# Holding back small bfloat16 products and telling a list scheduler what a change of product kind costs, in a two-layer graph attention kernel

## The chip, the cores and the metric

The kernel runs on one core of one Trainium2 chip. The metric is device time in microseconds (us) of one execution. The time before is the median of seven runs, 916.81 us (912.74 to 923.02).

## The reference, cut to what matters

The input is a dense matrix `adj` of 2708 x 2708 in which few entries are not zero (the diagonal, and entries that grow denser towards low row and column numbers), and features `x` of 2708 x 256. Two layers follow each other. Layer 0 is a gated graph layer:

```python
node_support = node_adj_norm @ h                      # one plain aggregation
edge_output = _gru_cell(node_support, h, ...)
for each of 3 heads:                                  # _gat_head
    att = softmax(where(edge_adj > 0, e_plus, where(edge_adj < 0, e_minus, NEG_INF)), axis=1)
    edge_support += att * edge_adj @ (h @ W)
node_output = _gru_cell(edge_support / 3, h, ...)
x = layernorm(x + de * edge_output + dn * node_output)
```

Every softmax row has its denominator: the sum of the weights `exp(e)` over the entries of that row that are not zero, for each of the three heads. Layer 1 is an ordinary graph attention layer with four heads and a mask `adj > 0.5`, with a second layernorm behind it.

## The kernel before, in words

The kernel never multiplies with the whole matrix. It reads the matrix once, finds which rows hold anything in each block of columns, and then gathers only those rows. There are three stretches of work.

*Reading and listing* (first 240 us or so). SyncE loads `adjT` in blocks of 128 x 512 (tile `at`). ScalarE makes sign masks from it (`over`, `mask`, bfloat16), VectorE finds the non-empty rows (`f_found`), TensorE multiplies the masks in bfloat16 into banks `acc` and `db`. Between them TensorE also makes float32 products of `x` with the GRU weights, which are kept for later (`keep`). `listed` and `spread` turn the found rows into lists of row numbers (`f_idx`), with small bfloat16 products into banks `ls` and `pl`.

*Layer 0.* The columns are cut into 43 chunks of 64, and each chunk into "tiles" of up to 128 listed rows: 181 tiles in all, 163 of them gathered. For a tile n, `fetch_raw` brings the 128 x 64 entries of `adjT` and `fetch_rows` the 128 x 264 rows of features and weights (ring `rows`), each by an indirect DMA that GpSimd (POOL) issues. `prepared` makes `four` (the entries times 1 and times the three heads' weights, float32) and the mask `m0` (sign, bfloat16; its rows in the profile carry the short name `m`). `multiplied` makes two float32 products per tile into the bank `sums[c]` (acc; the profile records four matmuls for these two products) and one small bfloat16 product of mask and weights, 128 x 64 by 128 x 9, into the bank `dens[c]` (db): the denominators. There are two banks of each kind, taken in turn by the chunks. After the last tile of a chunk `divided` sums and inverts the denominators on VectorE, spreads them with one float32 product (`rden_own`) and scales the chunk. After every eight chunks (512 columns) `cells_and_norm` runs the GRU cells: 12 products with `f_gat_w`, 24 for each cell (half of that where `keep` has done a part), transposes, the layernorm, and the projection for layer 1, whose rows go to a table in DRAM.

*Layer 1.* Once its table is written, 91 gathered tiles (indirect DMAs into the same ring `rows`) are weighed on VectorE, multiplied in float32 and finished. The masks of these tiles are 91 further indirect DMAs of 128 x 128 entries (`fetch_mask`, tile `raw1`, in the profile `raw<-in_adj_dram`). They need only the lists, so they can be issued during layer 0.

The order of the instructions on each engine isn't that of the source. Class `Plan` records every instruction, and `Plan.issue` is a list scheduler: it gives each recorded operation a cost from `Plan.cost`, follows the dependencies that buffers make, and at each step lets the engine that is free first issue the ready operation with the longest remaining chain (`tail`). What it decides is written into the program; on the chip each engine then works through its queue in that order. All instructions of the fast path therefore stand at one line in the profile, L208. A general path for other inputs stands behind a branch and doesn't run.

Consecutive TensorE instructions with the same output bank are joined to one operation of the scheduler (up to 16 of them). The cost of a product before is one line:

```python
t = max(0.06, n / 2000) if ins[0].dtype == BF16 else max(0.22, n / 590)
```

Of the kernel before, what the change touches and what calls it, by code (L numbers as in the profile page):

```python
# [11 lines left out]
BF16 = mybir.dt.bfloat16  # L12
# [8 lines left out]
P = 128  # L21
# [4 lines left out]
C1 = D // HEADS1  # L26
# [15 lines left out]
W0 = 64  # L42
# [54 lines left out]
class Plan:  # L97
# [8 lines left out]
    ENGINES = ("tensor", "vector", "scalar", "gpsimd", "sync")  # L106
    LAG = 0.08
    LOAD, RATE, QUEUED = 2.2, 250.0e3, 4.0
    TABLES = {AF.Sigmoid: 1, AF.Tanh: 1, AF.Exp: 2, AF.Sqrt: 3}

    def __init__(self, nc):
# [36 lines left out]
    def cost(self, engine, method, out, ins, kwargs):  # L148

        n = max(self.count(v) for v in [out] + ins)  # L150
        if method == "indirect_dma_start":
            return 1.25, 3.0
        if method == "dma_start":
            size = 4
            for _, k in tuple(out.ap):
                size *= k
            return 0.08 if engine == "sync" else 0.25, self.LOAD + size / self.RATE
        if engine == "tensor":
            n = self.count(out)
            t = max(0.06, n / 2000) if ins[0].dtype == BF16 else max(0.22, n / 590)  # L160
            return t, t + 0.1
        by_partition = any(isinstance(kwargs.get(k), bass.AP) for k in ("bias", "scale"))
        if engine == "scalar":
            t = 0.09 + n / 1200 + 0.1 * by_partition
        elif engine == "gpsimd":
            t = 0.1 + n / (1300 if method == "memset" else 320)
        elif method == "reciprocal":
            t = 0.07 + n / 160
        else:
            pairs = all(v.dtype == BF16 and tuple(v.ap)[-1] == (1, 2) for v in [out] + ins)  # L170
            t = 0.06 + n / (1900 if pairs else 3800 if method == "memset" else 960)
            t += 0.065 * (method == "scalar_tensor_tensor")
        return t, t + 0.08

    def note(self, engine, method, f, args, kwargs):
        found = list(args) + list(kwargs.values())
        found = [v.ap if isinstance(v, bass.IndirectOffsetOnAxis) else v for v in found]
        found = [v for v in found if isinstance(v, bass.AP)]
        out, ins = found[0], found[1:]
        writes = [out] + ([kwargs["accum_out"]] if kwargs.get("accum_out") is not None else [])  # L180
        n, deps = len(self.ops), set()

        last = self.ops[-1] if n else None
        joined = (
            engine == "tensor" and n and last.engine == engine and last.out == out.tensor.name
            and len(last.calls) < self.JOINED
        )
        n -= joined
        for v in found:
            t = self.touched(v)  # L190
            if t is None:
                continue
            name, p0, p1, m = t
            w = any(v is o for o in writes)
            old = self.seen.setdefault(name, [])
            keep = []
            for other in old:
                k, q0, q1, mo, wo = other
                if (w or wo) and k != n and p0 < q1 and q0 < p1 and m & mo:
                    deps.add(k)  # L200
                    if w and p0 <= q0 and q1 <= p1 and not mo & ~m:
                        continue
                keep.append(other)
            keep.append((n, p0, p1, m, w))
            self.seen[name] = keep
        busy, done = self.cost(engine, method, out, ins, kwargs)
        table = self.TABLES.get(args[2] if method == "activation" else None, 0)
        call = lambda: f(*args, **kwargs)  # L208
        if joined:
            last = self.ops[n]  # L210
            deps.discard(n)
            last.calls.append(call)
            last.deps |= deps
            last.busy += busy
            last.done += busy
            return
        self.ops.append(Op(engine, [call], busy, done, table, deps, method, self.urgent, out.tensor.name))

    def issue(self):
        ops, total = self.ops, len(self.ops)  # L220
        after = [[] for _ in ops]
        for n, op in enumerate(ops):
            for k in op.deps:
                after[k].append(n)
        tail, urgent = [0.0] * total, [op.urgent for op in ops]
        for n in reversed(range(total)):
            op = ops[n]
            for m in after[n]:
                tail[n] = max(tail[n], tail[m] + (0.0 if ops[m].engine == op.engine else self.LAG))
                urgent[n] = max(urgent[n], urgent[m])  # L230
            tail[n] += op.done
        tail = [t + u for t, u in zip(tail, urgent)]
        left = [len(op.deps) for op in ops]
        start = [0.0] * total
        free = dict.fromkeys(self.ENGINES, 0.0)
        ready = {e: [] for e in self.ENGINES}
        for n, op in enumerate(ops):
            if not left[n]:
                ready[op.engine].append(n)
        moved, table = 0.0, 0  # L240
        for _ in range(total):
            t, e = min((max(free[e], min(start[n] for n in ready[e])), e) for e in self.ENGINES if ready[e])
            n = max((n for n in ready[e] if start[n] <= t), key=lambda n: (tail[n], -n))
            ready[e].remove(n)
            op = ops[n]
            busy, done = op.busy, op.done
            if op.table and op.table != table:
                busy, done, table = busy + 1.3, done + 1.3, op.table
            free[e] = t + busy
            end = t + done  # L250
            if op.method == "dma_start":
                moved = max(moved, t + self.LOAD) + done - self.LOAD
                end = moved
                if e == "sync":
                    free[e] = max(free[e], moved - self.LOAD - self.QUEUED)
            for call in op.calls:
                call()
            for m in after[n]:
                same = ops[m].engine == e and "dma" not in op.method
                start[m] = max(start[m], end + (0.0 if same else self.LAG))  # L260
                left[m] -= 1
                if not left[m]:
                    ready[ops[m].engine].append(m)
        return max(free.values())
# [32 lines left out]
def fast_path(ctx: ExitStack, tc: tile.TileContext, i: dict, out: bass.AP, bad: bass.AP):  # L297
# [11 lines left out]
    nc = plan = Plan(tc.nc)  # L309
# [11 lines left out]
    H3 = 3 * HEADS0  # L321
# [15 lines left out]
    const = ctx.enter_context(tc.tile_pool(name="f_const", bufs=1))  # L337
# [100 lines left out]
    for t, of in ((less_room, TILES0 + TILES1), (less_whole, WHOLE0 + WHOLE1)):  # L438
        c = 0
        while c < len(of):  # L440
            e = c
# [3 lines left out]
            c = e  # L445
# [275 lines left out]
    for b in range(0, NF, 7):  # L721
        e = min(b + 7, NF)
# [17 lines left out]
    for b in range(0, NF, 7):  # L740
        e = min(b + 7, NF)
# [103 lines left out]
    for g, cs in enumerate(groups):  # L845
        w = width[g]
# [86 lines left out]
            xn[:p, b, :], xn[:p, b, :], mv[:p, b, 0:1], rstd[:p, b : b + 1], op0=ALU.subtract, op1=ALU.mult  # L933
        )

    rowp, sp = Rings(const, 8), Rings(const, 4)
    gp, zp = Rings(const, 2, home1), Rings(const, 1, home2)

    rows, ready = {}, {}
# [20 lines left out]
    def prepared(n):  # L960

        c, whole, m = work0[n]
        d0, w = spans[0][c]
        raw = raws.pop(n)
        four = sp.tile([P, 4 * W0], F32, name="four")
        a = four[:, :w]
        own = d0 - m * P
        if not whole:
            nc.vector.scalar_tensor_tensor(
                a, iota[:, :w], rel0[:, c, m : m + 1], raw, op0=ALU.not_equal, op1=ALU.mult  # L970
            )
        elif 0 <= own < P:
            nc.vector.tensor_mul(a, raw, off_diag[:, own : own + w])
        else:
            nc.vector.tensor_copy(a, raw)
        weight = of_rows(n)[1]
        for h in range(HEADS0):
            nc.scalar.activation(four[:, (h + 1) * w : (h + 2) * w], a, AF.Copy, scale=weight[:, h : h + 1])
        m0 = sp.tile([P, W0], BF16, name="m0")
        nc.scalar.activation(m0[:, :w], a, AF.Sign)  # L980

        if n % RAWS == RAWS - 1 or n == len(work0) - 1:
            k = n - n % RAWS
            of, at = (early, k) if k < EARLY else (home4, (k - EARLY) % 32)
            nc.vector.tensor_reduce(
                low[:, k // RAWS : k // RAWS + 1], of[:, at * W0 : (at + n - k + 1) * W0], AX.X, ALU.min
            )
        ready[n] = (four, m0)

    sums, dens = {}, {}  # L990

    def multiplied(n):
        c, whole, m = work0[n]
# [9 lines left out]
        for o in range(KD):  # L1003
# [1 line left out]
                sums[c][:, o * 4 * W0 : o * 4 * W0 + 4 * w], lhsT=xs[:, o * P : (o + 1) * P],  # L1005
                rhs=four[:, : 4 * w], start=start and o == 0, stop=stop, skip_group_check=True,
            )
        nc.tensor.matmul(
            dens[c][:w, :H3], lhsT=m0[:, :w], rhs=e3, start=start, stop=stop, skip_group_check=True
        )  # L1010
        rows.pop(n, None)
        return stop

# [780 lines left out]
```

## Time and profile before

| | |
|---|---|
| median of seven runs | 916.81 us (912.74 to 923.02) |
| the profiled execution | 922.55 us, its span 920.8 us |
| mean granted TensorE clock | 0.940 |
| TensorE (PE) busy | 811.4 us, 88% of the span |
| VectorE (DVE) busy | 613.7 us, 67% |
| ScalarE (ACT) busy | 538.8 us, 59% |
| GpSimd (POOL) busy | 529.5 us, 58% |
| TensorE bfloat16 products of the denominators | 180 recorded, of 181 tiles |
| indirect DMAs issued by POOL in the recording | 254 `rows`, 130 entries of layer 0 into `f_home`, 91 masks of layer 1 |

Busy time counts the recorded duration of instructions. Matmuls overlap with their neighbours, so the distance between the starts of two groups says more than the duration of one. On POOL an indirect DMA is recorded for the time in which its descriptors are made; the gap that follows each of them isn't counted as busy. PEclk is the clock that TensorE was granted, in tenths of full speed in the page and as a fraction in the tables by stretch.

### The profile page before, as it was taken

How to read it: one execution, taken by the hardware profiler on the slowest of the kernel's cores; microseconds unless marked ns; L12 is line 12 of the kernel's file. 1: busy time of each engine (PE TensorE's matmuls, PEld its weight loads, DVE VectorE, ACT ScalarE, POOL GpSimd, SP SyncE). 2: the span in 40 equal slices, each digit the busy share in tenths (PEclk: the TensorE clock that was granted, in tenths of full speed). 3: DMA queues.
4: the chain of work that ended last, by engine and by line, in shares of the span. 5: the costliest groups of instructions: out<-in, count | busy, mean ns of one | idle time of the engine just before them, and what ended most of it. 6: DMA issues, size and time to landing. Idle time of an engine off the chain costs nothing. (4 is left out here: it accounts for less than half of the span.)

```text
span 920.8 us, 13879 instructions
## 1 busy us (share of the span) xinstructions
PE 811.4 (88%) x3879; PEld 487.5 (53%) x3879; DVE 613.7 (67%) x2011; ACT 538.8 (59%) x1503; POOL 529.5 (58%) x613
## 2 busy tenths in 40 slices
PE   5897878879999999989999999999999776989970
PEld 3532333334566664657457556556544555777760
DVE  5475756874545746957486387398345656999995
ACT  3667677888578873848369558449413330334471
POOL 3007775000455787767777777777777606677720
PEclk9778998999999999979999999999999788999985
DMA  8677897885643332433265344343322313555513
GB/s 297 205 241 225 250 272 220 275 250 165 207 121 93 91 103 70 131 96 93 65 198 153 76 139 127 83 118 96 94 51 58 81 55 108 172 174 162 144 49 125
DMA packets 84303, 131.95 MB, mean 143 GB/s; under 512 B 21368, under 2 KB 43136, under 8 KB 83576
## 3 DMA queue, kind: packets, MB, share of 16 engines
q1 hardware_dynamic: 56056, 71.21, 25.1%
q0 software_dynamic: 20320, 45.59, 19.3%
q10 hardware_dynamic: 7840, 14.16, 4.2%
q8 instruction: 33, 0.54, 0.3%
q14 instruction: 54, 0.44, 0.2%
HBM read 109.79 MB, written 21.12 MB: 142 GB/s over the span
## 5 line engine op out<-in xcount | busy, mean ns | idle before, releaser
L208 POOL DMA_INDIRECT rows<-f_T,f_idx x254 | 252.2, 993 | 140.5 <-issue 47.2
L208 PE MATMUL acc<-four,rows 128*128 128x256 f32 (+1 forms) x712 | 195.1, 403 | 4.5 <-ACT four L208 2.7
L208 ACT ACTIVATE four<-four,rows 128x64 f32<-128x64 f32 (+1 forms) x534 | 144.9, 337 | 18.6 <-DMA rows<-f_T,f_idx 16.8
L208 POOL DMA_INDIRECT f_home<-in_adjT_dram,f_idx x130 | 132.5, 1019 | 39.6 <-issue 26.2
L208 PEld LDWEIGHTS acc<-four,rows 128*128 128x128 f32 x712 | 126.6, 193 | 29.1 <-ACT four L208 8.2
L208 POOL DMA_INDIRECT raw<-in_adj_dram,f_idx x91 | 89.2, 980 | 32.7 <-issue 16.5
L208 DVE TENSOR_REDUCE f_found<-f_home 128x16 f32<-128x1024 f32 (+5 forms) x84 | 72.2, 883 | 14.5 <-DMA f_home<-in_adjT_dram 9.0
L208 ACT ACTIVATE f_home<-f_home,f_minus_half 128x1024 bf16<-128x1024 f32 (+4 forms) x72 | 69.7, 976 | 16.8 <-PE db L208 9.5
L208 ACT ACTIVATE f_home<-f_home 128x1024 bf16<-128x1024 f32 (+4 forms) x72 | 63.0, 882 | 20.7 <-PE acc L208 14.5
L208 PE MATMUL acc<-f_home,rows 128*65 128x128 f32 (+1 forms) x480 | 64.8, 287 | 11.0 <-DVE f_home L208 11.0
L208 PEld LDWEIGHTS acc<-f_home,rows 128*65 128x65 f32 x480 | 52.6, 143 | 18.7 <-DVE f_home L208 13.4
L208 ACT ACTIVATE m<-four 128x64 bf16<-128x64 f32 (+1 forms) x181 | 41.0, 248 | 32.5 <-PE db L208 21.3
L208 PE MATMUL side<-f_home,f_node_wi 128*128 128x512 f32 (+1 forms) x144 | 59.4, 547 | 0.2
L208 DVE SCALAR_TENSOR_TENSOR f_home<-pl,rows,f_m 128x128 f32<-128x128 f32 x196 | 53.8, 340 | 6.8 <-DMA rows<-f_T,f_idx 6.4
L208 PE MATMUL side<-f_home,f_edge_wi 128*128 128x512 f32 (+1 forms) x144 | 58.0, 544 | 0.0
L208 PE MATMUL db<-f_home,f_only 128*22 128x512 bf16 (+2 forms) x132 | 42.0, 405 | 17.8 <-ACT f_home L208 17.7
L208 PE MATMUL side<-f_home,f_gat_w 128*128 128x512 f32 (+1 forms) x144 | 55.6, 542 | 1.2 <-DVE f_home L208 1.2
L208 PE MATMUL db<-f_home,rows 128*65 128x128 f32 x376 | 51.8, 287 | 4.1 <-DVE f_home L208 3.6
L208 DVE TENSOR_TENSOR f_home<-f_home,side 128x512 f32<-128x512 f32 (+1 forms) x56 | 36.4, 654 | 25.9 <-PE side L208 24.6
L208 DVE SCALAR_TENSOR_TENSOR four<-f_iota,f_rel,f_home 128x64 f32<-128x64 f32 (+1 forms) x130 | 35.8, 278 | 26.5 <-PE acc L208 19.1
L208 POOL TENSOR_TENSOR f_home<-f_home,f_off_diag 128x128 f32<-128x128 f32 (+1 forms) x22 | 12.2, 573 | 69.4 <-ACT f_home L208 69.4
L208 DVE TENSOR_SCALAR f_m<-raw 128x128 uint8<-128x128 f32 (+1 forms) x91 | 20.8, 240 | 42.6 <-DMA raw<-in_adj_dram,f_idx 42.3
(207 smaller groups left out, 1461.5 us busy)
## 6 DMA issues: line engine op xcount, KB each, us to landing
f_home<-in_adjT_dram SPq DMA_DIRECT2D x50, 512.0 KB
f_XH<-kept ACTq DMA_DIRECT2D x48, 256.0 KB
f_home<-f_XH SPq DMA_DIRECT2D x48, 256.0 KB
f_home<-f_TS SPq DMA_DIRECT2D x5, 1024.0 KB
rows<-f_T SPq DMA_DIRECT2D x31, 132.0 KB
rows<-f_T,f_idx POOLq DMA_INDIRECT x254
f_T<-f_home SPq DMA_DIRECT2D x21, 132.0 KB
f_xn<-in_x_dram SPq DMA_DIRECT2D x3, 896.0 KB
```

Of the source, the lines that this page charges most:

```text
L208: call = lambda: f(*args, **kwargs)
```

## The change: what it does

In layer 0 the small bfloat16 product of a tile is no longer issued with the tile. It is put on a list and issued when four have come together or the chunk ends, one behind the other into the same bank, so that they become one operation of the scheduler. For this the masks `m0` get eight buffers in place of four and the ring `rows` nine in place of eight, since a tile's rows and mask are held until its product is issued.

The scheduler learns two things. A float32 product whose stationary operand is wider than 65 columns costs at least 0.43 us in place of 0.22. And TensorE now has a "kind", as ScalarE had a function table: a change between float32 and bfloat16 is charged 0.2 us, and in the choice of the next operation one of the other kind counts as if its remaining chain were 5 us shorter. ScalarE's charge of 1.3 us for a table is as before.

```diff
+    SWITCH, STAY = {"scalar": 1.3, "tensor": 0.2}, {"tensor": 5.0}
...
-            t = max(0.06, n / 2000) if ins[0].dtype == BF16 else max(0.22, n / 590)
+            if ins[0].dtype == BF16:
+                t = max(0.06, n / 2000)
+            else:
+                t = max(0.22 if ins[0].ap[-1][1] <= C1 + 1 else 0.43, n / 590)
...
+        if engine == "tensor":
+            table = 1 + (ins[0].dtype == BF16)
...
-        moved, table = 0.0, 0
+        moved, tables = 0.0, dict.fromkeys(self.ENGINES, 0)
...
-            n = max((n for n in ready[e] if start[n] <= t), key=lambda n: (tail[n], -n))
+            other = lambda n: ops[n].table not in (0, tables[e])
+            n = max((n for n in ready[e] if start[n] <= t), key=lambda n: (tail[n] - self.STAY.get(e, 0.0) * other(n), -n))
...
-            if op.table and op.table != table:
-                busy, done, table = busy + 1.3, done + 1.3, op.table
+            if other(n):
+                busy, done, tables[e] = busy + self.SWITCH[e], done + self.SWITCH[e], op.table
...
-    rowp, sp = Rings(const, 8), Rings(const, 4)
+    rowp, sp = Rings(const, 9), Rings(const, 4)
+
+    COUNTED = 4
...
-        m0 = sp.tile([P, W0], BF16, name="m0")
+        m0 = sp.tile([P, W0], BF16, name="m0", bufs=2 * COUNTED)
...
-    sums, dens = {}, {}
+    sums, dens, counted = {}, {}, []
...
-        nc.tensor.matmul(
-            dens[c][:w, :H3], lhsT=m0[:, :w], rhs=e3, start=start, stop=stop, skip_group_check=True
-        )
+        counted.append((start, stop, m0[:, :w], e3))
+        if stop or len(counted) == COUNTED:
+            for first_of, last_of, mask, weights_of in counted:
+                nc.tensor.matmul(
+                    dens[c][:w, :H3], lhsT=mask, rhs=weights_of, start=first_of, stop=last_of,
+                    skip_group_check=True,
+                )
+            counted.clear()
```

Since the scheduler decides anew with other costs, the order on all engines changes with it. The number of instructions of each kind on TensorE and the number of indirect DMAs stay the same.

## The prediction

> **What bounds the kernel now.** I read the busy time by stretch first, with the stretches cut where layer 0's 1st, 52nd, 84th, 108th, 132nd and 156th gathers of `rows` stand (52 gathered tiles belong to the first group of eight chunks, 32 to the second, then 24, 24, 24), and the last one ending with the last mask gather of layer 1. Columns: stretch, its length, then busy time and instructions of PE, PEld, DVE, ACT, POOL, granted clock, DMA share, GB/s.
>
> ```profile
> 242.00:327.30 85.30, 82.13 (x449) 55.19 (x447) 48.32 (x170) 66.08 (x253) 55.27 (x56) 1.00 0.40 117
> 327.30:422.70 95.40, 89.59 (x411) 53.53 (x410) 65.78 (x196) 56.81 (x189) 72.04 (x67) 0.93 0.37 97
> 422.70:500.30 77.60, 77.51 (x313) 46.94 (x312) 50.95 (x158) 52.07 (x184) 57.84 (x60) 1.00 0.46 134
> 500.30:568.60 68.30, 67.52 (x236) 38.06 (x236) 44.53 (x136) 42.54 (x141) 50.69 (x51) 1.00 0.42 116
> 568.60:638.40 69.80, 68.93 (x249) 40.34 (x248) 48.28 (x159) 43.58 (x144) 52.73 (x53) 1.00 0.37 98
> 638.40:739.20 100.80, 93.74 (x321) 53.60 (x320) 52.69 (x192) 37.69 (x108) 73.00 (x76) 0.93 0.29 73
> ```
>
> TensorE is busy for 303.6 of the 311.1 us of the four middle stretches: it ends them. POOL looks three quarters used. The timeline of POOL says otherwise:
>
> ```profile
> 439.27 0.94 POOL L208 DMA_INDIRECT f_home<-in_adjT_dram,f_idx  x1 [0.30 <-issue]
> 440.51 0.94 POOL L208 DMA_INDIRECT f_home<-in_adjT_dram,f_idx  x1 [0.30 <-issue]
> 441.76 0.94 POOL L208 DMA_INDIRECT f_home<-in_adjT_dram,f_idx  x1 [0.30 <-issue]
> ```
>
> A gather takes 0.94 us and 0.30 us lie behind it whatever it waits for, so POOL can issue one every 1.25 us and no more. With 0.30 us for each instruction the middle stretches hold 72.0 + 19.8, 57.8 + 17.7, 50.7 + 15.3 and 52.7 + 15.9 = 301.9 us of POOL work in 311.1. POOL is as full as TensorE. What lets TensorE lead is what POOL does: 23 of its 228 gathers there are masks for layer 1, which nobody needs before 763 us, where layer 1's first row gather starts. They fill gaps.
>
> What the change is aimed at stands in TensorE's timeline (start, length, what):
>
> ```profile
> 484.96 1.13 PE L208 MATMUL acc<-four,rows 128*128 128x256 f32 x4
> 486.02 0.19 PE L208 MATMUL db<-rows,m 128*64 128x9 bf16 x1
> 486.14 1.99 PE L208 MATMUL acc<-four,rows 128*128 128x256 f32 x8
> 488.07 0.59 PE L208 MATMUL db<-rden_own,f_ones_f 64*128 64x192 f32 x2
> ...
> 490.83 0.26 PE L208 MATMUL db<-rows,m 128*64 128x9 bf16 x3
> 491.02 0.44 PE L208 MATMUL side<-f_ident,f_xn 128*128 128x128 f32 x2
> ```
>
> From start to start, a tile's four float32 matmuls take 486.02 - 484.96 = 1.06 us with a break of kind on both sides, eight take 1.93, so four more cost 0.87. The bfloat16 product takes 0.12. A tile with its own bfloat16 visit costs 1.18, without it 0.87: a visit costs 0.31 us. Three in one visit take 0.19, so each further product costs about 0.035. A visit that is merged into another saves 0.31 - 0.035, about 0.28 us.
>
> **The change part by part.** *Visits.* I counted the visits to bfloat16 (uninterrupted runs of such products) in the order in which the instructions stand before and after. They fall from 203 to 91. By stretches of the TensorE queue, cut at the first `f_gat_w` product of each group's cells: 97 to 60, 33 to 12, 28 to 6, 19 to 6, 19 to 5, 6 to 1. That is 112 x 0.28 = 31 us of TensorE time. If TensorE ended every stretch, this would be the gain.
>
> *The gathers.* The same comparison on POOL shows what moves. Between the 52nd and the 156th row gather there stand 256 gathers after the change where 228 stood before: 104 rows as before, 100 entries of layer 0 for 101, and 52 masks for 23. By stretch 77 for 65, 65 for 59, 56 for 51, 58 for 53. The scheduler now believes TensorE slower (0.2 us per change of kind, 0.43 us for each small float32 product, where two transposes of 128 x 128 take 0.27 us together, 491.02 to 491.29), sees POOL free for longer, and fills it with masks. But on the chip the queue is in order, and each mask stands ahead of a row that a tile waits for. After the last row gather 39 masks are left, where 65 were.
>
> So, for the four middle stretches: TensorE needs 303.6 less 70 visits x 0.28 = 284 us. POOL needs 301.9 + 28 x 1.25 = 337 us. POOL now ends them, and they last 26 us longer than 311.1. Even with every gather at 1.25, 257 instructions (one small addition is among them) last 321 us: 10 us more than now.
>
> *The first stretch* (242 to 327 us). POOL has 55.3 + 16.8 = 72.1 us of work in 85.3 and one gather more; TensorE is the bound. Of the 37 visits fewer up to the first cells, 27 are of the denominators and lie here: 27 x 0.28 = 7.6 us. Against it stands the ring: up to four of nine rows are held until their products are issued, so five can be ahead where eight could. POOL's waits for released rows are within the 13 us that it has free here. The gain is 0 to 7.6; I take 5, nearer to TensorE's row, since that engine is busy for 96% of the stretch.
>
> *The lag at the end.* Now the 156th row gather starts at 637.40 and the last long block of cells at 652.65, 15.2 us later: TensorE works off a backlog. With POOL late there is no backlog. In the new order the denominators of the next chunk (rows 157 to 159) stand before these cells, so 3 x 1.25 us, then 2.75 from issue to use (the gather at 393.76 released ScalarE at 396.51), 0.87 until the product starts (397.38) and 1 for the product: 8.4, call it 9. Saved: 6 us.
>
> *The rest.* Before 242 us ten visits go, 2.8 us, in a stretch that TensorE ends only in its last 40 us; against it, mask products held back by the 5 us of preference hold their buffers longer. From -3 to +5; I take -1, by the visits, the only part with a row. Behind 652 us five visits go: -1.4 us. The cells there, 52 us of float32 products alone, are the same, and layer 1 has the same gathers and VectorE work (102.17 us busy of the 105 from 800 to 905). More buffers cost no time. ScalarE's 49 table loads become 45, hidden in its idle time.
>
> Sum: -5 + 26 - 6 - 1 - 1.4 = +12.6 us. Against the profiled execution (922.55 us, span 920.8, 1.75 around it) that is 935; that execution lies 5.7 us above the median, and I carry the difference to the median of 916.81: 929.
>
> A rule that speaks against the change: the row first. At 393 to 397 us TensorE waited 3.37 us for rows; from 400 to 410 its granted clock was 0.50 and four float32 matmuls, from 397.38 to 399.30, took 1.92 us for 1.06. The Trainium skill, "TensorE: Matmul & The Clock Gate", Part 1, says that an idle window of about 3.4 us brings the half clock and as much activity lifts it. By the row I count no such event more; by the rule, with 337 - 284 = 53 us of idle TensorE in the middle stretches, each wait over 3.4 us adds several us at half clock, an estimate of some 6 for one like that at 397, and the sum would be near 20 with one more.
>
> **The rivals.** *TensorE ends it all the same and the kernel is faster.* For it: 98% busy now, 31 us less to do. POOL bounds it: from the first row gather at 242.1 to the 159th there stand 317 POOL instructions, 316 x 1.25 = 395, so 637.1, and 4.6 more to the cells: 641.7 for 652.65. With the 2.4 of the rest that is 13.4 us less, if POOL never waits and no gather is longer (in the second stretch they take 72.04 us for 66, 1.09 each). Every us of POOL's surplus over 1.25 per instruction takes one off. That surplus is now 396 - 285 x 1.25 = 40 us, 22 of it waits; my sum comes to 26. The rival decides below 9 us of surplus; I price it at 4 us: 916.8 - 9 = 908. *The two cancel*: a surplus of about 13 us, 917. *The grouping doesn't reach the chip*: excluded, the visits are counted in the order itself. *Two queues block each other*: on top of POOL's 337 us come waits as long as now (311.1 - 301.9 = 9 us), the first stretch gains nothing (5): 929 + 14 = 943.
>
> **How the numbers follow.** POOL ends the middle stretches, slower, 0.50 (its own range 921 to 938); with both queues blocking, 0.17 at 943; cancelled, 0.15 at 917; TensorE's gain up to POOL's floor, 0.18 at 908. A measurement of this kernel can tell about 0.5%, 4.6 us, from no change: faster 0.18, same 0.15, slower 0.67. The range reaches from 908 to 944.
>
> **What would show it.** Right: in the profile after, between the 52nd and 156th row gather, POOL with gaps of 0.30 us throughout and over 325 us long; TensorE busy there for less than 93%, waiting for DMA of `rows` or for `four`; about 91 bfloat16 visits; the 156th row gather at 645 us or later; the end of layer 1 shifted by the same amount. Wrong: the last long block of cells before 650 us, TensorE still at 98%, or POOL's gathers closer than 1.25 us. If layer 1 itself (763 to 905) changes length by over 5 us, the sum missed a part.

## The result and the profile after

The changed kernel takes 925.14 us in the median of 26 runs (916.42 to 932.87), the kernel before 917.38 (911.04 to 924.66, 63 runs over all comparisons). The ratio is 1.0081, 95% interval 1.0063 to 1.0099: slower by 0.8%, some 7 to 8 us.

The profiled execution doesn't show this difference: 921.9 us after and 922.55 before, spans 919.8 and 920.8. The one before was a long one of its kind (5.2 us above the median), the one after a short one (3.2 below). So the two traces tell where time moved. They can't say where each of the last few microseconds went.

The page after, its span and the busy times (share of the span, instructions):

```profile
span 919.8 us, 13865 instructions
PE 795.0 (86%) x3879; PEld 486.1 (53%) x3879; DVE 613.2 (67%) x2011; ACT 531.6 (58%) x1499; POOL 523.7 (57%) x613
```

TensorE is busy for 16 us less than before (811.4), and the time is not shorter. Busy time by stretch, for the four middle stretches, cut about 1 us behind the same gathers as before (the 52nd row gather is at 312.1 us, the 156th at 650.4). Columns: stretch, length, then busy time and instructions of PE, PEld, DVE, ACT, POOL, granted clock, DMA share, GB/s:

```profile
313.10:417.40 104.30, 90.08 (x468) 56.67 (x466) 71.95 (x216) 62.45 (x211) 80.70 (x78) 0.98 0.37 98
417.40:505.00 87.60, 83.04 (x294) 50.77 (x295) 52.59 (x165) 50.78 (x179) 63.62 (x65) 0.90 0.43 120
505.00:576.70 71.70, 64.88 (x235) 36.82 (x233) 46.24 (x141) 40.80 (x138) 54.64 (x56) 1.00 0.43 116
576.70:651.30 74.60, 68.89 (x235) 39.98 (x236) 48.89 (x162) 41.47 (x143) 56.97 (x58) 0.95 0.37 98
```

Against the four stretches before, each is longer: by 8.9, 10.0, 3.4 and 4.8 us. TensorE stood idle for 7.5 of 311.1 us; now it does for 31.3 of 338.2. The granted clock was 0.93, 1.00, 1.00, 1.00 and is 0.98, 0.90, 1.00, 0.95. In both traces the clock's records are either 1.0 or 0.5. Time at 0.5 in the middle stretches went from 13.7 us (one spell, from 397.5 on) to 27.2 (four spells: 3.4 us from 357.8, 6.8 from 419.2, 10.2 from 480.6, 6.8 from 630.8). POOL looks as forecast. Its timeline (start, length, what, the gap ahead; all instructions stand at L215 here, since the helper has moved by a few lines):

```profile
622.31 1.12 POOL L215 DMA_INDIRECT raw<-in_adj_dram,f_idx  x1 [0.30 <-DVE f_m L215]
623.73 0.94 POOL L215 DMA_INDIRECT raw<-in_adj_dram,f_idx  x1 [0.30 <-issue]
624.98 0.95 POOL L215 DMA_INDIRECT rows<-f_T,f_idx  x1 [0.30 <-issue]
```

Masks of layer 1 (`raw`) stand directly ahead of rows of layer 0, with the 0.30 us gap. With 0.30 us per gather the four stretches hold 104.1, 83.1, 71.4 and 74.4 us of POOL work: full, but for 4.5 us in the second.

What TensorE waited for from 322 to 660 us (columns: total us, times, longest; the window lies 10 us later than the gathers, since TensorE works behind them) is only in part what was forecast:

```profile
PE acc L215 <- ACT four L215: 9.9, 9, 3.0
PE side L215 <- DVE f_home L215: 5.4, 7, 1.1
PE acc L215 <- DVE f_home L215: 4.9, 6, 3.2
PE db L215 <- DVE rden_own L215: 4.2, 5, 1.4
PE side L215 <- ACT f_xT L215: 2.9, 2, 1.8
PE side L215 <- DVE f_xn L215: 2.4, 5, 0.8
...
PE db L215 <- DMA rows<-f_T,f_idx: 0.2, 1, 0.2
```

A row's DMA is among them once, with 0.2 us. Some 10 us are for `four`; the rest, two thirds of the listed time, are other results of VectorE and ScalarE. In the kernel before (339 to 653 us) the view lists these two lines and 1.2 us of others:

```profile
PE db L208 <- DMA rows<-f_T,f_idx: 3.4, 1, 3.4
PE acc L208 <- ACT four L208: 1.7, 3, 0.8
```

And the thing that was aimed at, in TensorE's timeline:

```profile
554.69 2.86 PE L215 MATMUL acc<-four,rows 128*128 128x256 f32 x12 [0.48 <-DVE f_home L215]
557.48 0.35 PE L215 MATMUL db<-rows,m 128*64 128x9 bf16 x6
557.76 1.13 PE L215 MATMUL acc<-four,rows 128*128 128x256 f32 x4
559.18 0.59 PE L215 MATMUL db<-rden_own,f_ones_f 64*128 64x192 f32 x2 [0.29 <-DVE rden_own L215]
```

Twelve float32 products stand in one run, then six bfloat16 products take 0.28 us from start to start (557.48 to 557.76), where one took 0.12. A further product costs 0.03 us. The merging works as costed, and beside it stand waits that were not there.

### The profile page after: what moved, and what is told of

Same layout as the page of the kernel before. It is cut to its first block, busy times and chain, and to the rows that moved or that the text cites. A ratio compares the mean times of both kernels' runs of the same rounds, so it can differ in the third digit from the quotient of the medians.

```text
span 919.8 us, 13865 instructions
## 1 busy us (share of the span) xinstructions
PE 795.0 (86%) x3879; PEld 486.1 (53%) x3879; DVE 613.2 (67%) x2011; ACT 531.6 (58%) x1499; POOL 523.7 (57%) x613
## 5 line engine op out<-in xcount | busy, mean ns | idle before, releaser
L215 POOL DMA_INDIRECT rows<-f_T,f_idx x254 | 252.5, 994 | 163.7 <-issue 85.3
L215 PE MATMUL acc<-four,rows 128*128 128x256 f32 (+1 forms) x712 | 193.8, 411 | 18.2 <-ACT four L215 11.8
L215 ACT ACTIVATE four<-four,rows 128x64 f32<-128x64 f32 (+1 forms) x534 | 145.9, 337 | 45.7 <-DMA rows<-f_T,f_idx 28.3
L215 PEld LDWEIGHTS acc<-four,rows 128*128 128x128 f32 x712 | 134.0, 200 | 57.0 <-ACT four L215 20.1
L215 POOL DMA_INDIRECT f_home<-in_adjT_dram,f_idx x130 | 129.7, 998 | 41.8 <-issue 23.2
L215 POOL DMA_INDIRECT raw<-in_adj_dram,f_idx x91 | 89.8, 986 | 30.6 <-issue 17.2
L215 DVE TENSOR_REDUCE f_found<-f_home 128x16 f32<-128x1024 f32 (+5 forms) x84 | 71.8, 883 | 22.2 <-DMA f_home<-in_adjT_dram 11.2
L215 PE MATMUL acc<-f_home,rows 128*65 128x128 f32 (+1 forms) x480 | 66.5, 292 | 18.1 <-DVE f_home L215 16.8
L215 ACT ACTIVATE f_home<-f_home,f_minus_half 128x1024 bf16<-128x1024 f32 (+4 forms) x72 | 69.9, 977 | 11.3 <-DMA f_home<-in_adjT_dram 4.2
L215 ACT ACTIVATE f_home<-f_home 128x1024 bf16<-128x1024 f32 (+4 forms) x72 | 63.1, 882 | 21.4 <-POOL f_home L215 11.5
L215 PEld LDWEIGHTS acc<-f_home,rows 128*65 128x65 f32 x480 | 52.5, 144 | 29.0 <-DVE f_home L215 21.5
L215 PE MATMUL side<-f_home,f_node_wi 128*128 128x512 f32 (+1 forms) x144 | 61.3, 558 | 3.2 <-DVE f_home L215 3.1
L215 DVE SCALAR_TENSOR_TENSOR f_home<-pl,rows,f_m 128x128 f32<-128x128 f32 x196 | 54.2, 340 | 6.7 <-DMA rows<-f_T,f_idx 6.0
L215 PE MATMUL side<-f_home,f_gat_w 128*128 128x512 f32 (+1 forms) x144 | 55.8, 544 | 2.0 <-DVE f_home L215 2.0
L215 PE MATMUL side<-f_home,f_edge_wi 128*128 128x512 f32 (+1 forms) x144 | 57.5, 543 | 0.0
L215 DVE SCALAR_TENSOR_TENSOR four<-f_iota,f_rel,f_home 128x64 f32<-128x64 f32 (+1 forms) x130 | 35.1, 277 | 27.5 <-PE acc L215 22.1
L215 PE MATMUL db<-f_home,rows 128*65 128x128 f32 x376 | 48.3, 278 | 5.0 <-DVE f_home L215 5.0
L215 PE MATMUL db<-f_home,f_only 128*22 128x512 bf16 (+2 forms) x132 | 40.7, 389 | 12.2 <-ACT f_home L215 11.1
L215 ACT ACTIVATE m<-four 128x64 bf16<-128x64 f32 (+1 forms) x181 | 40.4, 247 | 13.5 <-DVE four L215 11.7
L215 DVE TENSOR_TENSOR f_home<-f_home,side 128x512 f32<-128x512 f32 (+1 forms) x56 | 36.4, 655 | 15.4 <-PE side L215 15.1
L215 PE MATMUL acc<-f_home,f_home 128*9 128x512 bf16 (+2 forms) x132 | 40.4, 387 | 7.2 <-ACT f_home L215 7.1
L215 DVE SCALAR_TENSOR_TENSOR f_home<-ls,rows,f_m 128x128 f32<-128x128 f32 (+1 forms) x168 | 45.9, 337 | 0.2 <-DMA rows<-f_T,f_idx 0.2
```

## The experiments

Each kernel is timed against the kernel before on the same chip. "Middle" is the time from layer 0's 52nd to its 156th row gather, the four stretches above.

**Is POOL the bound? Masks held back.** The first masks of layer 1 go where they went before (26 may be issued early), or none may; the others wait in the scheduler until layer 0's last row gather. Prices and code are otherwise as after the change; the scheduler decides the rest of the order anew, as in every kernel below. The diff is that of the first kernel; the second has `self.held[0:]`.

```diff
+        for n in self.held[26:]:
+            after[self.gate].append(n)
+            left[n] += 1
...
+            plan.gate = len(plan.ops)
             gathered(rows[n], T0, idx0[:, c, m : m + 1], 0)
...
+        plan.held.append(len(plan.ops))
         gathered(r[:, :w], adj, idx1[:, c, m : m + 1], d0)
```

> The changed kernel, but all mask gathers of layer 1 except the first 26 are held in the scheduler until the last row gather of layer 0 stands: POOL's queue has 231 gathers between the 52nd and 156th row gather (228 before, 256 in the changed kernel), TensorE's has 90 bfloat16 visits as in the changed kernel. Theory (masks ahead of rows in POOL's in-order queue): that stretch needs 306 us of POOL and 284 of TensorE, so it lasts 306 to 312 us where the changed kernel takes 338; the time is 895 to 905 us. Rival (the holding back itself costs: rows held in the ring, denominators late): no gain, 917 to 930. Rival (the preference for one kind spoils TensorE's order): as the changed kernel, 920 to 930.

> The changed kernel with all 91 mask gathers held until layer 0's last row gather: 205 gathers in the middle stretches. Theory: POOL needs 274 us there and TensorE 284, TensorE ends them again, 285 to 295 us; behind the last row gather stand 91 x 1.27 = 115 us of masks, which may delay layer 1's first row gather by some 5 us; time 880 to 895 us. Rival (holding back costs): 915 to 930. Rival (preference spoils the order): 920 to 930.

Measured: 928.02 us, ratio 1.0148 (1.0093 to 1.0203), with the masks as before; 932.15, 1.0194 (1.0138 to 1.0249), with all masks last. The stretches with all masks last:

```profile
307.20:408.00 100.80, 87.11 (x460) 55.84 (x459) 72.09 (x213) 62.73 (x211) 76.62 (x74) 0.99 0.36 99
408.00:495.00 87.00, 79.72 (x301) 49.26 (x300) 50.10 (x149) 51.30 (x177) 49.95 (x53) 0.93 0.39 112
495.00:569.20 74.20, 69.04 (x231) 39.37 (x229) 44.74 (x133) 40.85 (x137) 48.69 (x51) 0.93 0.36 104
569.20:641.00 71.80, 66.22 (x242) 38.77 (x242) 46.69 (x139) 41.41 (x144) 28.70 (x30) 1.00 0.27 76
```

In the last three stretches POOL has 45 instructions fewer (134 for 179). With 0.30 us for each POOL is now free for 21, 10 and 34 us. The three last 233.0 us, after the change 233.9. With the masks as before it is the same in the last stretch: 37 gathers for 58, and 74.4 us for 74.6. TensorE is idle for 31.7 us of the middle with all masks last, 31.3 after the change. Nor do the rows come late to TensorE by way of ScalarE, which needs them to make `four`. ScalarE's waits for rows in the middle fall by 8 us with all masks last (second line, after the change first), to less than the 11.3 us before, and TensorE's waits for `four` stay (third line, 322 to 660 us with all masks last):

```profile
ACT four L215 <- DMA rows<-f_T,f_idx: 19.0, 19, 3.7
ACT four L216 <- DMA rows<-f_T,f_idx: 10.8, 13, 1.7
PE acc L216 <- ACT four L216: 9.7, 10, 2.2
```

So in these three stretches POOL's full queue is not what makes them long. In the first of the four POOL is full in both kernels (76.62 + 74 x 0.30 = 98.8 of 100.8): it has few masks there to give up (5 after the change), and whether POOL sets its length stays open. In all the kernels timed here POOL is full in that stretch but for at most 4 us, and the stretch is longer where more gathers stand in it: 91 to 97 us with 65 or 66 of them, 99 to 107 with 71 to 77, some 114 with 82 or 83. That is what a bound by POOL would look like, and also what a queue that is filled would. It is worth at most the 8.9 us by which that stretch grew.

**Which part costs? Pricing without holding back, and holding back without pricing.** Pricing alone has `COUNTED = 1`, four `m0` and eight `rows` buffers, with all three prices kept. Holding back alone keeps the list of four and the buffers, with the prices of before:

```diff
-    SWITCH, STAY = {"scalar": 1.3, "tensor": 0.2}, {"tensor": 5.0}
+    SWITCH, STAY = {"scalar": 1.3, "tensor": 0.0}, {"tensor": 0.0}
...
-                t = max(0.22 if ins[0].ap[-1][1] <= C1 + 1 else 0.43, n / 590)
+                t = max(0.22, n / 590)
```

> The changed kernel without holding back: each tile's bfloat16 product is offered with its tile (COUNTED = 1, four masks, eight rows), the prices and the preference stay. 136 visits (202 before, 90 in the changed kernel), 268 gathers in the middle stretches. Theory: POOL needs 302 + 40 x 1.27 = 353 us there, so slower than the changed kernel: 932 to 945 us. Rival (holding back costs): without it faster than the changed kernel, 905 to 917. Rival (preference spoils the order): about as the changed kernel, 922 to 930.

> The changed kernel with the old prices: products held back up to four, no charge and no preference for a kind, small float32 products at 0.22. 126 visits, 226 gathers in the middle stretches. Theory: TensorE needs 303.6 - 51 x 0.28 = 289 us there, POOL 299, so about 300 to 305 us for 311 before; time 903 to 912 us. Rival (holding back costs): 922 to 935. Rival (preference spoils the order): below before as well, 900 to 912.

Measured: pricing alone 957.29 us, 1.0461 (1.0397 to 1.0526), so the prices cost more without the holding back than with it. Holding back alone 906.92 us, 0.9896 (0.9834 to 0.9958): faster than both kernels of this case. (Its additional buffers come with it; they were not tried apart.) Its stretches:

```profile
320.00:411.00 91.00, 85.30 (x427) 53.24 (x427) 67.78 (x204) 58.16 (x193) 70.81 (x67) 0.98 0.37 102
411.00:486.20 75.20, 72.25 (x292) 43.97 (x291) 48.01 (x149) 47.75 (x170) 56.74 (x59) 0.98 0.47 135
486.20:555.00 68.80, 66.03 (x244) 38.94 (x244) 46.14 (x141) 42.60 (x145) 52.11 (x51) 1.00 0.41 115
555.00:623.10 68.10, 65.94 (x244) 38.99 (x243) 46.64 (x153) 42.23 (x144) 52.29 (x52) 1.00 0.37 101
```

The middle lasts 303.0 us for 311.7, with TensorE idle for 13.6 us and its clock at 0.98 to 1.00. From the first cells' `f_gat_w` products to the fifth block of them there are 48 visits to bfloat16, where 99 were before: 51 x 0.28 = 14.3 us, and TensorE's busy time in the middle falls from 304.1 to 289.4, by 14.7. (A part of this is the clock: 6.8 us at half clock here, 13.7 before. If TensorE was busy in them, that is worth some 3 us, and 11 are left for the visits.) What TensorE waited for is shorter too (327 to 636 us):

```profile
PE acc L215 <- ACT four L215: 4.0, 6, 1.2
PE side L215 <- DVE f_home L215: 2.4, 2, 1.4
```

POOL is full here as well: 70.81 + 67 x 0.30 = 90.9 of 91.0 us, then 74.4, 67.4 and 67.9 of 75.2, 68.8 and 68.1, though the middle is shorter than in the kernels above. A queue that is full at 303 us and also at 338 can't by itself tell what sets either length. In this version two of the four stretches hold no mask at all, the others 6 and 16; whether POOL sets its length was not tried.

**Which price?** Each price was put alone on the version that only holds back, and the preference was taken away from the full change:

```diff
     preference alone, cost max(0.22, n / 590):
+    SWITCH, STAY = {"scalar": 1.3, "tensor": 0.0}, {"tensor": 5.0}
     0.43 us alone, cost as after the change:
+    SWITCH, STAY = {"scalar": 1.3, "tensor": 0.0}, {"tensor": 0.0}
     charge alone, cost max(0.22, n / 590):
+    SWITCH, STAY = {"scalar": 1.3, "tensor": 0.2}, {"tensor": 0.0}
     all but the preference, cost as after the change:
+    SWITCH, STAY = {"scalar": 1.3, "tensor": 0.2}, {"tensor": 0.0}
```

> Holding back with the old prices, plus only the preference of 5 us for the kind that runs (no charge, small float32 products at 0.22): 98 visits where holding back alone has 126, 234 gathers in the middle stretches. The theory of POOL's queue has fallen with the two runs that moved the masks; three parts of the pricing are left. Theory A (the preference lets denominators and list products wait until TensorE runs dry, so banks come free late): 916 to 930 us, TensorE idle over 20 us between the 52nd and 156th row gather. Theory B (the price of 0.43 us for small float32 products is wrong and shifts the order) and theory C (the charge of 0.2 us does): no slower than holding back alone, 900 to 910.

> Holding back, plus only the price of 0.43 us for float32 products with a wide stationary operand: 130 visits, 235 gathers in the middle stretches. Theory A: as holding back alone, 903 to 911. Theory B: 915 to 928. Theory C: 903 to 911.

> Holding back, plus only the charge of 0.2 us for a change of kind: 125 visits, 238 gathers in the middle stretches. Theory A: as holding back alone, 902 to 911. Theory B: the same. Theory C: 914 to 928.

> The changed kernel with the preference of 5 us set to 0; holding back, the charge of 0.2 and the price of 0.43 stay: 135 visits, 251 gathers in the middle stretches, nearly as many as in the changed kernel. Theory A: the loss goes, 902 to 912. Theory B and theory C: it stays, 918 to 930.

Measured, with lengths read from each trace (us; idle is the middle's length less TensorE's busy time in it; layer 1 runs from its first row gather to the end of the span):

| kernel | ratio to before | first row gather at | middle | TensorE idle in it | gathers in it | layer 1 |
|---|---|---|---|---|---|---|
| before | 1 | 242.1 | 311.7 | 7.6 | 228 | 157.5 |
| holding back alone | 0.9896 (0.9834 to 0.9958) | 240.4 | 303.0 | 13.6 | 226 | 156.9 |
| + 0.43 us | 0.9956 (0.9934 to 0.9978) | 237.3 | 317.7 | 23.4 | 235 | 151.1 |
| + charge | 1.0010 (0.9970 to 1.0051) | 242.2 | 317.9 | 20.3 | 238 | 156.9 |
| + preference | 1.0037 (1.0002 to 1.0072) | 247.5 | 320.6 | 22.0 | 234 | 157.2 |
| + 0.43 us and charge | 1.0108 (1.0079 to 1.0137) | 233.2 | 333.7 | 34.6 | 251 | 153.0 |
| all: the change | 1.0081 (1.0063 to 1.0099) | 230.5 | 338.2 | 31.3 | 256 | 152.0 |
| pricing alone | 1.0461 (1.0397 to 1.0526) | 232.0 | 361.8 | 41.0 | 268 | 156.1 |

In these traces every price, alone, makes the middle longer by 15 to 18 us against holding back alone, and TensorE's idle time in it longer by 7 to 10. The lengths are of one execution each. The one with the charge took 924.71 us, 7.6 above the median of its kernel, so a part of its 15 us may be that execution; the others lie within 5.2 us of theirs. By the times, charge and preference are clear of holding back alone; for the 0.43 us alone the intervals overlap. The 0.43 us and the charge together make it 31 us longer. The gathers in the middle follow its length. The preference is the one part that shows no cost on top of the other two: 1.0081 with it, 1.0108 without, intervals that overlap.

The 0.43 us also gives something back, in two places for which the prediction had next to nothing. The first row gather comes earlier, most so with the other prices beside it (229 to 233 us). And layer 1, here with 0.43 us alone and then with holding back alone, is shorter by some 5.9 us, with the same instructions:

```profile
760.40:911.40 151.00, 114.08 (x938) 96.98 (x938) 138.89 (x570) 59.51 (x219) 87.30 (x91) 0.92 0.46 141
```

```profile
746.10:903.00 156.90, 116.21 (x938) 98.88 (x938) 138.34 (x570) 59.41 (x219) 86.89 (x91) 0.87 0.45 136
```

**Is it VectorE's queue?** After the change VectorE waits longest for gathers of layer 0's entries: its reductions over them (into `f_low`) stand in the queue, and may stand ahead of work that TensorE waits for. From the 52nd to 156th row gather these waits take 39.8 us after the change, 15.6 before and 11.6 with holding back alone. In these kernels such a reduction may only be issued behind the VectorE instructions that use its eight tiles: in the change, in the version that only holds back, and in the kernel before.

```diff
+        deps |= self.also
+        self.also = set()
...
+        plan.read[n] = len(plan.ops)
...
+            plan.also = {plan.read[j] for j in range(k, n + 1)}
             nc.vector.tensor_reduce(
```

> The changed kernel, with one more rule in the scheduler: the guard's reduction over eight gathered tiles (f_low, on VectorE) may stand in VectorE's queue only after the instructions there that use these eight tiles, so that it never waits for a gather. In the changed kernel VectorE waits 39.8 us for gathers before these reductions in the middle stretches (holding back alone 11.6, before 15.6). Theory D (prices make TensorE look slow, the reductions are put where the scheduler believes the gathers landed, and on the chip VectorE's queue stands there): the loss goes, 898 to 912 us, VectorE's wait at f_low near 0, middle stretches 300 to 315 us. Theory E (the waits are spread over all queues, since the scheduler's clock for TensorE is slow against the other engines' too cheap prices): only a part goes, 915 to 922. If the reductions are beside the point: 922 to 930.

> Holding back with the old prices, and the same rule for f_low. Theory D: VectorE's 11.6 us at f_low go, a gain of 0 to 8 us on holding back alone, 897 to 907. Theory E: 898 to 909, hardly to be told apart. It is the candidate for a version faster than both kernels.

> The kernel before with the same rule for f_low alone. Theory D and theory E: TensorE is busy for 98% of the middle stretches there, so little is to be had: 908 to 918 us. With the run of the changed kernel under this rule it tells whether the rule helps any kernel or repairs what the prices did.

Measured: the change with this rule 927.44 us, 1.0124 (1.0097 to 1.0151); holding back with it 908.91, 0.9919 (0.9892 to 0.9947); the kernel before with it 920.87, 1.0037 (1.0011 to 1.0063). VectorE's longest line of waits from 309 to 656 us, first in the change, then in the change with the rule:

```profile
DVE f_low L215 <- DMA f_home<-in_adjT_dram,f_idx: 39.8, 10, 9.7
```

```profile
DVE f_home L218 <- PE side L218: 49.2, 13, 11.7
```

The reductions' waits for gathers are gone (the masks of layer 1 are still waited for, 11.9 us for 6.6), and the middle is 346.7 us long in place of 338.2, with TensorE idle for 36.6. VectorE now waits for TensorE instead. The rule by itself costs the kernel before 0.4% and gives the change nothing, so these waits are not what the change loses by. The pair without prices is of use for another reason: under the same rule, holding back stands at 0.9919 against 1.0037, a gain of 1.2%, where it is 1.0% without the rule. So its gain was seen in two different orders.

**Are VectorE and ScalarE priced too low beside a dearer TensorE?** The full change, with the fixed part of VectorE's and ScalarE's costs raised:

```diff
-            t = 0.09 + n / 1200 + 0.1 * by_partition
+            t = 0.15 + n / 1200 + 0.1 * by_partition
...
-            t = 0.07 + n / 160
+            t = 0.14 + n / 160
...
-            t = 0.06 + n / (1900 if pairs else 3800 if method == "memset" else 960)
+            t = 0.14 + n / (1900 if pairs else 3800 if method == "memset" else 960)
```

> The changed kernel with the scheduler's fixed prices of VectorE raised from 0.06 and 0.07 to 0.14 us and of ScalarE from 0.09 to 0.15, which brings them to the recorded durations (128 x 512 addition: 0.59 before, 0.67 now, 0.68 recorded; 128 x 64 product with three inputs 0.19, 0.27, 0.277). Theory E (relative clocks): TensorE's waits for VectorE and ScalarE go, 903 to 917 us. Theory D: the reductions still stand too early, since gathers keep their price: 918 to 930.

Measured: 936.16 us, 1.0200 (1.0166 to 1.0234). The middle has 339.5 us with 29.8 of idle TensorE, no better, and layer 1 grows to 159.2. As an explanation of the loss this falls too, at least in the form of one raised constant for all their instructions.

## Why the prediction was right in size and wrong in cause

**The whole.** 929 was forecast, +12.6 us; the medians differ by 7.8. The sign and the range hold. In the two profiled executions the terms add up to -1.0; with the 5.2 us by which the one before lies above its median and the 3.2 by which the one after lies below, that is the 7.8 but for rounding:

| term | forecast | measured |
|---|---|---|
| before the first row gather (242.1 to 230.5) | -1 | -11.6 |
| first stretch, to the 52nd row gather (83.6 to 81.6) | -5 | -2.0 |
| middle (311.7 to 338.2) | +26 | +26.6 |
| lag to the last long block of cells (15.2 to 9.9) | -6 | -5.3 |
| from there to layer 1 (110.7 to 107.5) | -1.4 | -3.2 |
| layer 1 (157.5 to 152.0) | 0 | -5.5 |

That the total came near is luck in good part: the middle's +26 was met though POOL doesn't set its last three stretches, and the two ends took off 17 us where the sum had 1.

**The visits: right in the main.** 0.28 us per merged visit was forecast. Six products in 0.28 us, and 14.7 us of busy time for 51 visits in the version without prices (some 11 without the clock's part, for 14.3), bear it out. The stretches that the prediction lists add up to 202 and 90 visits, not 203 and 91, and the traces show 24 and 20 table loads on ScalarE, not 49 and 45; the differences, 112 and 4, stand.

**"POOL now ends them": wrong, with the right number.** This is the step that failed: the 28 gathers more were counted as time that the stretches need. Forecast were 337 us by counting 256 gathers, and 338.2 came. Nearly all signs that the prediction named for POOL were there: gaps of 0.30 us, over 325 us, TensorE at 306.9 / 338.2 = 91%, the 156th row gather at 650.4. (One was not: that gather came 13.0 us later, layer 1 started 4.5 us later and its end did not shift in the profile.) They were signs of a queue that is full, and masks that nobody needs yet can fill it. The two kernels with the masks taken away show POOL idle for up to 34 us of a stretch and the three last stretches as long as ever. In place of POOL, TensorE's own waits fill the middle, 31 us for 8. Only in the first of the four stretches, which grew by 8.9 us, may POOL set the length. The number of gathers may stand for how long the scheduler believed TensorE to need, and that the chip needed as long is a coincidence as far as these runs show. The sign that could have told cause from filler was the waits of TensorE. `four` is on them, as the prediction said, but rows only with 0.2 us, and two thirds of the listed time is for other results of VectorE and ScalarE.

**What the middle's 26.5 us are.** TensorE's idle time grew by 31.3 - 7.6 = 23.7 us. The 70 visits fewer should have taken 19.6 us off its busy time, which instead rose from 304.1 to 307.0: 22.5 us are to be explained. The time at half clock rose by 13.5 us, worth half of that, some 7, if TensorE was busy in it. 1232 products are recorded in these stretches for 1209, an estimate of 5 us at the 0.22 us of a small one. The remaining 11 or so are open.

**The clock: costed at nothing, and not nothing.** "By the row I count no such event more" was wrong. TensorE ran at half clock for 27.2 us in place of 13.7, though the longest listed single wait of TensorE is 3.2 us. What the Trainium skill says in "TensorE: Matmul & The Clock Gate", Part 1, that idle windows of some 3.4 us bring the half clock, points the right way here. But single waits as long as that were not needed: ahead of the four spells of half clock, within 7 us, the longest waits are 3.0, 3.2, 1.4 and 0.6 us.

**The first stretch and the two ends: mis-sized.** The first stretch gave 2.0 of the 5 us forecast: TensorE is idle there for 6.3 of 81.6 us at a clock of 0.96, where it was 3.2 of 85.3 at 1.00. For the time before the first row gather and for layer 1 the prediction had -1 and 0; they gave -11.6 and -5.5. It said that layer 1 moving by over 5 us would mean that the sum missed a part, and it did: how long layer 1 takes also hangs on the price of a small float32 product. With that price alone layer 1 takes 151 us for 157, and in five other kernels with it 151 to 153; in two with it, it doesn't (pricing alone, 156.1, and the dearer VectorE, 159.2). No kernel without it came below 156.8. The granted clock differs too (0.92 in layer 1 with that price alone, 0.87 with holding back alone); which of the two follows from the other is not shown.

**The rivals.** "TensorE ends it and the kernel is faster" is what the holding back does by itself: 906.92 us, where the rival stood at 908. It lost to the pricing that came with it. Behind the first row gather the prediction weighed the prices only for what they put on POOL, not for what they do to the order on TensorE, VectorE and ScalarE.

**What stays open.** Why each price makes TensorE wait longer. What the runs show is that each does, by its idle time in one trace each, and that three explanations don't hold: masks ahead of rows (in the last three stretches), reductions ahead of the cells' work on VectorE, and too low a fixed price of the other engines. Not tried: a bfloat16 product with wider masks, holding back alone with fewer early masks, and fewer gathers in the first stretch under the same prices.

## What to carry to other kernels

A queue that is full of movable filler is no proof of a bound: ask who waits for its results, and take the filler away to see whether the time falls. A change that regroups work and also teaches the scheduler new prices is two changes, to be timed apart; here the first gains 1.0% (0.4 to 1.7%) and the second takes more than that away. A price that is nearer to the measured duration of one engine's work need not give a better order (the charge of 0.2 us is nearer to a visit's 0.31 than nothing, and it cost time; the 0.43 us is not nearer for every product, since two transposes of 128 x 128 take 0.27 us together), so each price has to earn its place on the chip.

## What the runs showed of the hardware

One visit of TensorE from float32 to a bfloat16 product and back costs 0.31 us, each further product in it 0.03 (three products in 0.19 us before, six in 0.28 after the change). TensorE can fall to half clock without a wait of 3.4 us: after the change four spells of 3.4 to 10.2 us, 27 us together, stand behind waits of at most 3.2 us, one of them behind 1.4 us. It need not: the kernel before with the rule for the reductions has 13.0 us of idle TensorE in its middle, in waits of up to 1.7 us, and no half clock there. In no kernel did two indirect gathers on POOL start less than 1.24 us apart, and about three quarters of them start 1.23 to 1.27 us apart (0.94 and 0.30), also where POOL had idle time (all masks last).
